# A dense layer stream issued in paced portions beside pair attention, with constant products in thinly filled slots

## The chip, the cores and the metric

The kernel runs on one core of a Trainium2 chip. The metric is the device time of one execution in microseconds. A core has five engines that work side by side, each with its own instruction queue: TensorE (PE, matrix products; PEld are its weight loads), VectorE (DVE), ScalarE (ACT), GpSimd (POOL) and SyncE (SP, which here issues the DMA transfers). Each queue runs in order, and an instruction that waits holds everything behind it on its engine.

## The reference, cut to what matters

Two layers are computed on x of 4 x 1024 tokens with 256 channels. The first (a recurrent mixer and a mixture of experts) is the first 1100 us and is not touched. The second is pair attention and a dense feed-forward layer, and the change is in how these two are interleaved.

```python
def _L1_attn_ref(X, Wq, Wk, Wphi, Wy_w, Wy_b, We_w, We_b):
    q = jnp.einsum('bnc,ac->bna', X, Wq)
    k = jnp.einsum('bnc,ac->bna', X, Wk)
    Vy = jnp.einsum('bnc,dc->bnd', X, Wy_w) + Wy_b
    e = jax.nn.relu(_rho_signed_sqrt(q[:, :, None, :] + k[:, None, :, :]))
    scores = jnp.einsum('bija,a->bij', e, Wphi)
    m = jnp.max(scores, axis=-1, keepdims=True)
    ex = jnp.exp(scores - m)
    ...
def _L1_ffn_ref(x, ...):                       # D_IN 256, D_HID 1024
    h = jax.nn.silu(_tlin(x, w1_w, w1_s)) * _tlin(x, w2_w, w2_s)
    h = jax.nn.gelu(_tlin(h, h1_w, h1_s), approximate=False)
    h = jax.nn.gelu(_tlin(h, h2_w, h2_s), approximate=False)
    return _tlin(h, w3_w, w3_s)
...
x = x + ga * _L1_attn_ref(h, ...)
h = _layernorm(x, axis=-1) * (1 + cb) + sb
x = x + gb * _L1_ffn_ref(h, ...)
```

## The kernel before, in words

**Blocks and turns.** pair_attention() handles 128 score blocks of 32 queries against all 1024 keys of a batch entry, 32 blocks for each of the four entries. A block is 16 tiles of 128 x 1024 in 8 pairs. Its loop runs 8 turns, p = 0 to 7, and each turn does one pair of the current block: weigh() on DVE (L1478, two passes over 128 x 1024), then work(ROOM[p]), then begin() and make() for a pair some 13 turns ahead. begin() puts the key sums on POOL (L1402, L1407), make() puts the others on ACT (L1427) or DVE (L1416), takes the square root on ACT (L1428) and the scores on PE (L1432, sixteen 32-column products). RING = 14 buffers hold the pairs between begin() and weigh(), so POOL can start a pair only when DVE has weighed one.

**The ends of a block.** At p = 5 top() takes the row maximum of the next block's scores (L1442, then a small product L1445 across partitions), at p = 6 exps() reads it (L1449), takes the exponential on ACT (L1451), and spread() copies the result over partitions on PE (L1458). exps() ends with switch(), which runs the Silu and Gelu activations that are waiting (L1375), so that ScalarE changes its function table only there: once in 8 turns.

**Work beside the blocks.** work(room) first calls tick(), which runs evictions whose LATE = 2 turns have passed, then takes generators from two lists, tasks and stream, until room is used up. A generator yields what it has issued, in units of one product of 128 x 128 by 256 columns, or nothing when it wants to wait a turn. ROOM is (4, 6, 6, 6, 6, 4, 3, 6). tasks holds finish(), which every four blocks puts the attention's output together (L1491, L1529, L1541; 14 units). stream holds first_rest() (the rest of the first layer), prepare() for each further batch entry, and dense(j) for the 16 groups of 256 tokens. Two PSUM banks serve all of these; banks[0] counts the free ones. finish() holds one for about eight turns.

**A dense group** goes through five matrices: W1 (16 units, gate() and first_products(), L1263, scaled by L1255, then Silu), W2 (16 units, multiplied with the Silu by L1298), H1 and H2 (64 units each, L1333, scaled by L1317, then Gelu), W3 (16 units, L1354, L1364, the sum L1365 and the store L1366). Activations sit in two tiles wide[0] and wide[1]; the input of W1 and W2 lies in a quarter of wide[1], and so the gate is split over both tiles. Between the matrices the group waits until its evictions are issued (while late) and its activation has run (while waiting). While a group is in H2, head() of the following one loads its tokens (L1268), normalises them (L920 to L947) and issues the first half of W1; the other half follows in dense().

**Weights** come in 512 KB tiles through weights() (L1047, on SP's queue), up to three ahead in four buffers. W1 and W2 are two tiles each, H1 and H2 eight each, W3 two.

A group can start when finish() has written its 256 tokens, every eight blocks. There is no other limit on the stream's speed than ROOM, the banks and the waits.

Of the kernel before, what the change touches and what calls it, by code (L numbers as in the profile page):

```python
# [14 lines left out]
P = 128  # L15
# [11 lines left out]
FB = 256  # L27
# [5 lines left out]
ROOM = (4, 6, 6, 6, 6, 4, 3, 6)  # L33
LATE = 2
ADDS = ('ap', 'pp', 'pp', 'dp', 'pp', 'ap', 'dp', 'ap')
# [799 lines left out]
def pair_attention(tc, a, link, out, cols_of, seen, ident):  # L835
# [14 lines left out]
    with tc.tile_pool(name="at_k", bufs=1) as pk, tc.tile_pool(name="at_w", bufs=1) as wp, tc.tile_pool(  # L850
# [31 lines left out]
        ewt, ews = [], []  # L882
        for i in range(2):
            t = wp.tile([P, 4, P], F32, tag=f"ewt{i}", name=f"ewt{i}")
            nc.gpsimd.memset(t, 0.0)
            ewt.append(t)
            t = wp.tile([P, 4, 64], F32, tag=f"ew{i}", name=f"ew{i}")
            nc.gpsimd.memset(t, 0.0)
            ews.append(t)
# [354 lines left out]
        def gate(j, m):  # L1244


            while not banks[0]:
                yield
            hT, to = wide[1][:, 0:2, :], (wide[1][:, 4 + m : 6 + m, :] if m < 4 else wide[0][:, m : m + 2, :])
            ps = bank([P, 2, FB], "ff_ps")  # L1250
            first_products(ps, weights(j, W1 + m // 4, 1 if m < 4 else 3), m, hT)
            if m % 4 == 2:
                used(j, W1 + m // 4)
            scale = fs[:, m : m + 2, 0:1].to_broadcast([P, 2, FB])
            later(LATE, lambda: nc.vector.tensor_tensor(to, ps, scale, ALU.mult))  # L1255
            yield 4

        def first_products(ps, w, m, hT):
# [6 lines left out]
        def head(j):  # L1265

            heads[j] = tokens[j] = p2.tile([P, 2, C], F32, tag="res", name="res")
            nc.sync.dma_start(tokens[j], dst[j].rearrange("(t p) c -> p t c", p=P))  # L1268
            yield
            yield  # L1270
            yield from normed(tokens[j], 2, j * FB // T, 3, wide[1][:, 0:2, :])
            for m in (0, 2):
                yield from gate(j, m)
# [4 lines left out]

        def dense(j):
# [3 lines left out]
            hT, gate_row = two[:, 0:2, :], rows[b]  # L1283
            if j not in heads:
                yield from head(j)
            for m in (4, 6):
                yield from gate(j, m)
            while late:
                yield
            between(two[:, 4:8, :], AF.Silu)  # L1290
            between(one[:, 4:8, :], AF.Silu)
            while waiting:
                yield

            def up(ps, m):
                for h in range(2):
                    g = two[:, 4 + m + h, :] if m < 4 else one[:, m + h, :]
                    nc.vector.scalar_tensor_tensor(  # L1298
                        one[:, m + h, :], ps[:, h, :], fs[:, m + h, 1:2], g, ALU.mult, ALU.mult
                    )  # L1300

            for m in range(0, 8, 2):
# [3 lines left out]
                first_products(ps, weights(j, W2 + m // 4), m, hT)  # L1306
# [3 lines left out]
                yield 4  # L1310
            while late:
                yield
            following = None
            for li, base, of, to in ((2, H1, one, two), (3, H2, two, one)):

                def hidden(ps, m):
                    nc.vector.tensor_tensor(  # L1317
                        to[:, m : m + 2, :], ps, fs[:, m : m + 2, li : li + 1].to_broadcast([P, 2, FB]), ALU.mult
                    )

                if li == 3 and follower() is not None:
                    following = head(follower())
                    next(following)
                for m in range(0, 8, 2):
                    if m == 4 and following is not None:
                        next(following)
# [14 lines left out]
                while late:  # L1341
                    yield
                between(to, AF.Gelu)
                if following is not None:
                    yield from following
                while waiting:
                    yield
            while not banks[0]:
                yield
            ps = bank([P, 2, C], "out_ps")  # L1350
            w = [weights(j, W3 + i).rearrange("p (k n) -> p k n", k=4) for i in range(2)]
# [9 lines left out]
            def last():  # L1361
                fin, res = two[:, 2:4, :], tokens.pop(j)
# [384 lines left out]
```

## Time and profile before

| | us |
|---|---|
| median of 3 runs | 4834.72 (4834.62 to 4846.67) |
| profiled execution | 4844.85, its span 4843.1 |
| first L1451 (block 0) to last L1451 (block 127) | 1109.3 to 4671.1 |
| mean granted TensorE clock over the span | 0.915 |
| L1432 scores, PE, 16384 instructions | 1169.6 busy |
| L1333 H1 and H2, PE, 4096 instructions | 999.1 busy |
| L1478 weighing, DVE, 2048 passes | 2393.1 busy |
| L1428 square roots, ACT, 1024 | 1928.6 busy |
| L1402 and L1407, POOL | 1600.0 and 1421.4 busy |

A product in f32 is two MATMUL instructions, so 4096 of L1333 are 2048 products. In the rows of the profile each group of instructions is named by line, engine, operation, output and inputs; after the bar or in brackets stands how long the engine was idle before it and which engine released it. Spans of busy engines overlap, and the clock column is the share of full clock that TensorE was granted.

### The profile page before, as it was taken

The page shows a single profiled execution, that of the slowest core. Times are in us where ns is not written, and L with a number is a line of the kernel's source. Part 1 is how long each engine was busy: PE and PEld are TensorE (multiplying, and loading weights), DVE is VectorE, ACT ScalarE, POOL GpSimd, SP SyncE. Part 2 cuts the span into 40 slices and gives each one's busy share as a digit, 9 for nine tenths or more (in the row PEclk, how much of TensorE's full clock was granted, in tenths as well). Part 3 has the DMA queues.
Part 4 walks back from the last instruction along what each step waited for, and adds up shares of the span by engine and source line. Part 5 has one row for each costly group of instructions (what it writes and reads, how often), then busy time and mean ns, then how long its engine had stood idle before and what let it go on. Part 6 is the DMA issues. An engine that isn't in the chain of part 4 may idle for free. (4 is left out here: it accounts for less than half of the span.)

```text
span 4843.1 us, 76620 instructions
## 1 busy us (share of the span) xinstructions
PE 4253.5 (88%) x28714; PEld 2423.4 (50%) x28714; DVE 3881.2 (80%) x6834; ACT 3316.7 (68%) x3183; POOL 3573.9 (74%) x2942
## 2 busy tenths in 40 slices
PE   6899999986888889899897889898889899998888
PEld 1233333433335446555564556555446555555567
DVE  5899999767898888778877878878788878878771
ACT  2333233227888898778878878888788888878851
POOL 3544444337899898889888888888898888888840
PEclk8799999987889889999998999999899999999999
DMA  4344333441112123322222332222223322222223
GB/s 137 91 120 118 107 112 108 128 140 34 33 63 68 63 73 102 105 93 81 79 86 56 109 108 83 85 79 81 66 82 105 106 86 83 77 77 75 78 86 116
DMA packets 256965, 433.16 MB, mean 89 GB/s; under 512 B 71897, under 2 KB 142737, under 8 KB 256337
## 3 DMA queue, kind: packets, MB, share of 16 engines
q1 hardware_dynamic: 253520, 425.76, 28.3%
q8 instruction: 226, 3.70, 0.3%
q10 hardware_dynamic: 2880, 1.98, 0.1%
q14 instruction: 147, 1.20, 0.1%
q0 software_dynamic: 192, 0.52, 0.0%
HBM read 403.99 MB, written 40.93 MB: 92 GB/s over the span
## 5 line engine op out<-in xcount | busy, mean ns | idle before, releaser
L1478 DVE CUSTOM_DVE_ANT_0 s<-s,xb 128x1024 f32<-128x1024 f32 x2048 | 2393.1, 1213 | 63.9 <-PE xb L1458 47.1
L1428 ACT ACTIVATE s<-s 128x2048 f32<-128x2048 f32 x1024 | 1928.6, 1908 | 174.1 <-POOL s L1407 104.6
L1402 POOL TENSOR_SCALAR s<-kB,qt 128x1024 f32<-128x1024 f32 x1397 | 1600.0, 1151 | 281.8 <-DVE ew L1478 108.4
L1407 POOL TENSOR_SCALAR s<-s 128x1024 f32<-128x1024 f32 x1016 | 1421.4, 1399 | 89.1
L1432 PE MATMUL sc<-s,wsel 128*32 128x256 f32 x16384 | 1169.6, 411 | 332.8 <-ACT s L1428 331.6
L1333 PE MATMUL ff_ps<-wide,fw 128*128 128x256 f32 x4096 | 999.1, 393 | 25.1 <-ACT wide L1375 23.7
L1432 PEld LDWEIGHTS sc<-s,wsel 128*32 128x32 f32 x16384 | 456.7, 114 | 903.2 <-ACT s L1428 500.4
L1333 PEld LDWEIGHTS ff_ps<-wide,fw 128*128 128x128 f32 x4096 | 762.8, 193 | 231.3 <-issue 102.5
L741 POOL TENSOR_TENSOR kv<-vb,out_k 128x512 f32<-128x512 f32 x256 | 324.0, 1274 | 244.0 <-DVE state L809 167.4
L1427 ACT ACTIVATE s<-kB,qt 128x1024 f32<-128x1024 f32 x387 | 439.9, 1137 | 18.6 <-DMA kB<-kd 18.1
L616 PE MATMUL e_ps<-wd,hid 128*128 128x512 f32 x896 | 417.8, 613 | 7.0 <-DVE acc L599 4.5
L1458 PE MATMUL xb<-ex,pick 64*128 64x256 f32 x2048 | 320.8, 436 | 46.2 <-ACT ex L1451 46.0
L809 DVE TENSOR_TENSOR_SCAN state<-dec,carry,kv 128x512 f32<-128x512 f32 x256 | 326.2, 1274 | 23.4 <-ACT dec L796 17.5
L616 PEld LDWEIGHTS e_ps<-wd,hid 128*128 128x128 f32 x896 | 170.9, 196 | 233.1 <-issue 219.2
L1416 DVE TENSOR_SCALAR s<-kB,qt 128x1024 f32<-128x1024 f32 x264 | 285.9, 1085 | 0.0
L1263 PE MATMUL ff_ps<-wide,fw 128*128 128x256 f32 x1024 | 268.0, 411 | 17.7 <-DMA fw<-in_ffw_dram 17.0
L1458 PEld LDWEIGHTS xb<-ex,pick 64*128 64x128 f32 x2048 | 193.2, 204 | 180.2 <-ACT ex L1451 80.0
L1317 DVE TENSOR_TENSOR wide<-ff_ps,ffn_s 128x512 f32<-128x512 f32 x128 | 88.0, 687 | 212.2 <-PE ff_ps L1333 212.2
L1442 DVE TENSOR_REDUCE sc<-sc 128x1 f32<-128x256 f32 x128 | 55.1, 431 | 249.0 <-PE sc L1432 248.4
L801 ACT COPY carry<-state 128x1 f32<-128x1 f32 x255 | 47.9, 188 | 295.6 <-DVE state L809 295.3
L1263 PEld LDWEIGHTS ff_ps<-wide,fw 128*128 128x128 f32 x1024 | 200.2, 204 | 79.7 <-issue 35.9
L1451 ACT ACTIVATE ex<-sc,neg 128x256 f32<-128x256 f32 x128 | 60.7, 474 | 254.0 <-DVE neg L1449 252.6
(254 smaller groups left out, 4155.1 us busy)
## 6 DMA issues: line engine op xcount, KB each, us to landing
fw<-in_ffw_dram SPq DMA_DIRECT2D x361, 512.0 KB
vb<-vd SPq DMA_DIRECT2D x1024, 64.0 KB
lent<-vd SPq DMA_DIRECT2D x64, 514.0 KB
wd<-in_w_down_dram SPq DMA_DIRECT2D x28, 1024.0 KB
kB<-kd SPq DMA_DIRECT2D x32, 512.0 KB
lent<-in_We_dram SPq DMA_DIRECT2D x32, 512.0 KB
kd<-nd SPq DMA_DIRECT2D x24, 512.0 KB
vd<-out_v SPq DMA_DIRECT2D x8, 512.0 KB
```

The costliest lines, as they stand in the source:

```text
L616: nc.tensor.matmul(ps, hid[:, k, t * P : (t + 1) * P], wd[:, k, :], start=k == 0, stop=k == HID // P - 1)
L741: nc.gpsimd.tensor_mul(kv, vb[:, g % 2, :], ready[u]["k"][:, n // HN, :])
L809: nc.vector.tensor_tensor_scan(s[:, 1 : U + 1], dec, kv, c, ALU.mult, ALU.add)
L1263: nc.tensor.matmul(ps[:, h, :], w[:, k, o : o + P], hT[:, k, :], start=k == 0, stop=k == 1)
L1333: nc.tensor.matmul(ps[:, h, :], w[:, k * P : (k + 1) * P], of[:, k, :], start=k == 0, stop=k == 7)
L1402: nc.gpsimd.tensor_scalar(self.s[p][:, h, :], kB[self.b][i % 8], 1.0, self.query(i), ALU.mult, ALU.add)
L1407: nc.gpsimd.tensor_scalar(both, both, FLT_MAX, 0.0, ALU.min, ALU.max)
L1427: nc.scalar.activation(t[:, h, :], kB[self.b][i % 8], AF.Relu, bias=self.query(i))
L1428: nc.scalar.activation(t, t, AF.Sqrt, bias=EPS_RHO)
L1432: nc.tensor.matmul(self.sc[32 * j : 32 * j + 32, 0:256], wsel[:, g, 16 * (1 - s) : 16 * (1 - s) + 32], t[:, h, 256 * j : 256 * (j + 1)], s ...
L1458: nc.tensor.matmul(xb[:, 256 * j : 256 * (j + 1)], pick[q, j % 2, s, :], self.ex[q, :], start=True, stop=True)
L1478: nc.vector.tensor_tensor_reduce(t[:, h, :], t[:, h, :], self.xb[s], 1.0, 0.0, ALU.mult, ALU.add, ew[:, self.n % 4, col : col + 1])
```

## The change

It has four parts. The four gates of W1 are issued in one go, gates(), for the following group behind H2, in the same stretch; their input is a tile hT of its own, all of wide[1] holds the gate, and its Silu waits for the same switch() as H2's Gelu. The stream is paced: even() divides a layer's units by the turns up to a switch(), and work() gives the stream only as much as rate and credit allow; EVEN, HALF and HURRY bound the rate, HURRY when work is waiting or near the end. head() runs in a list of its own, side. And work() adds products on constants (ident times pick, or times zeros into the score tile) in turns where fewer than LEAST = 2 units were issued, while scores are still being made. Besides, one ewt tile instead of two, and the last scaling, sum and store in two halves.

```diff
--- before.py
+++ after.py
@@ -31,7 +31,9 @@
 RING = 14
 PREP = 12
 ROOM = (4, 6, 6, 6, 6, 4, 3, 6)
+EVEN, HALF, HURRY = 4.2, 3.3, 5.0
 LATE = 2
+LEAST = 2
 ADDS = ('ap', 'pp', 'pp', 'dp', 'pp', 'ap', 'dp', 'ap')
 FIRST_ON_SCALAR = 6
 LEAD = 2
@@ -879,11 +881,10 @@
         same = wp.tile([P, P], F32, tag="same", name="same")
         part = wp.tile([P, 4], F32, tag="part", name="part")
         pick = wp.tile([P, 2, 2, P], F32, tag="pick", name="pick")
-        ewt, ews = [], []
+        ewt, ews = wp.tile([P, 4, P], F32, tag="ewt", name="ewt"), []
+        nc.gpsimd.memset(ewt, 0.0)
+        hT = wp.tile([P, 2, FB], F32, tag="hT", name="hT")
         for i in range(2):
-            t = wp.tile([P, 4, P], F32, tag=f"ewt{i}", name=f"ewt{i}")
-            nc.gpsimd.memset(t, 0.0)
-            ewt.append(t)
             t = wp.tile([P, 4, 64], F32, tag=f"ew{i}", name=f"ew{i}")
             nc.gpsimd.memset(t, 0.0)
             ews.append(t)
@@ -1241,21 +1242,26 @@
 
         groups, heads, tokens = {}, {}, {}
 
-        def gate(j, m):
-
-
-            while not banks[0]:
-                yield
-            hT, to = wide[1][:, 0:2, :], (wide[1][:, 4 + m : 6 + m, :] if m < 4 else wide[0][:, m : m + 2, :])
-            ps = bank([P, 2, FB], "ff_ps")
-            first_products(ps, weights(j, W1 + m // 4, 1 if m < 4 else 3), m, hT)
-            if m % 4 == 2:
-                used(j, W1 + m // 4)
-            scale = fs[:, m : m + 2, 0:1].to_broadcast([P, 2, FB])
-            later(LATE, lambda: nc.vector.tensor_tensor(to, ps, scale, ALU.mult))
-            yield 4
-
-        def first_products(ps, w, m, hT):
+        def gates(j, n):
+
+            for m in range(0, 8, 2):
+                while not banks[0]:
+                    yield
+                ps = bank([P, 2, FB], "ff_ps")
+                first_products(ps, weights(j, W1 + m // 4, min(n, n + 1 - m // 4)), m)
+                if m % 4 == 2:
+                    used(j, W1 + m // 4)
+
+                def gated(ps=ps, m=m):
+                    scale = fs[:, m : m + 2, 0:1].to_broadcast([P, 2, FB])
+                    nc.vector.tensor_tensor(wide[1][:, m : m + 2, :], ps, scale, ALU.mult)
+                    if m == 6:
+                        between(wide[1], AF.Silu)
+
+                later(LATE, gated)
+                yield 4
+
+        def first_products(ps, w, m):
             w = w.rearrange("p (k n) -> p k n", k=2)
             for h in range(2):
                 o = (m + h) % 4 * P
@@ -1264,66 +1270,79 @@
 
         def head(j):
 
-            heads[j] = tokens[j] = p2.tile([P, 2, C], F32, tag="res", name="res")
+            tokens[j] = p2.tile([P, 2, C], F32, tag="res", name="res")
             nc.sync.dma_start(tokens[j], dst[j].rearrange("(t p) c -> p t c", p=P))
             yield
             yield
-            yield from normed(tokens[j], 2, j * FB // T, 3, wide[1][:, 0:2, :])
-            for m in (0, 2):
-                yield from gate(j, m)
+            yield from normed(tokens[j], 2, j * FB // T, 3, hT)
 
         def follower():
 
             return groups.get(stream[1]) if len(stream) > 1 else None
+
+        def even(units, most=EVEN, less=2):
+
+            t = turns[0]
+            end = t + 1 + (6 - t) % 8
+            if sum(g in groups for g in stream) > 2 or any(g not in groups for g in stream) or t > 8 * (N - 12):
+                most = HURRY
+            while units > most * (end - t - less):
+                end += 8
+            rate[0] = units / (end - t - less)
+            credit[0] = rate[0]
+
+        rate, credit, side = [0.0], [0.0], []
 
         def dense(j):
 
             b = j * FB // T
             one, two = wide
-            hT, gate_row = two[:, 0:2, :], rows[b]
+            gate_row = rows[b]
             if j not in heads:
+                heads[j] = True
                 yield from head(j)
-            for m in (4, 6):
-                yield from gate(j, m)
-            while late:
-                yield
-            between(two[:, 4:8, :], AF.Silu)
-            between(one[:, 4:8, :], AF.Silu)
-            while waiting:
+                even(16)
+                yield from gates(j, 3)
+                rate[0] = 0.0
+            while late or waiting:
                 yield
 
             def up(ps, m):
                 for h in range(2):
-                    g = two[:, 4 + m + h, :] if m < 4 else one[:, m + h, :]
                     nc.vector.scalar_tensor_tensor(
-                        one[:, m + h, :], ps[:, h, :], fs[:, m + h, 1:2], g, ALU.mult, ALU.mult
+                        one[:, m + h, :], ps[:, h, :], fs[:, m + h, 1:2], two[:, m + h, :], ALU.mult, ALU.mult
                     )
 
+            rate[0] = EVEN
             for m in range(0, 8, 2):
                 while not banks[0]:
                     yield
                 ps = bank([P, 2, FB], "ff_ps")
-                first_products(ps, weights(j, W2 + m // 4), m, hT)
+                first_products(ps, weights(j, W2 + m // 4), m)
                 if m % 4 == 2:
                     used(j, W2 + m // 4)
                 later(LATE, lambda ps=ps, m=m: up(ps, m))
                 yield 4
+            rate[0] = 0.0
             while late:
                 yield
-            following = None
+            follow = None
             for li, base, of, to in ((2, H1, one, two), (3, H2, two, one)):
 
                 def hidden(ps, m):
                     nc.vector.tensor_tensor(
                         to[:, m : m + 2, :], ps, fs[:, m : m + 2, li : li + 1].to_broadcast([P, 2, FB]), ALU.mult
                     )
-
-                if li == 3 and follower() is not None:
-                    following = head(follower())
-                    next(following)
+                    if m == 6:
+                        between(to, AF.Gelu)
+
+                if li == 3:
+                    follow = follower()
+                if follow is not None:
+                    heads[follow] = True
+                    side.append(head(follow))
+                even(*((64, EVEN) if follow is None else (80, HALF, 4)))
                 for m in range(0, 8, 2):
-                    if m == 4 and following is not None:
-                        next(following)
                     while not banks[0]:
                         yield
                     ps = bank([P, 2, FB], "ff_ps")
@@ -1338,17 +1357,18 @@
                         used(j, base + m + h)
                     later(LATE, lambda ps=ps, m=m: hidden(ps, m))
                     yield 2
-                while late:
-                    yield
-                between(to, AF.Gelu)
-                if following is not None:
-                    yield from following
-                while waiting:
+                if follow is not None:
+                    while side:
+                        yield
+                    yield from gates(follow, 1)
+                rate[0] = 0.0
+                while late or waiting:
                     yield
             while not banks[0]:
                 yield
+            rate[0] = EVEN
             ps = bank([P, 2, C], "out_ps")
-            w = [weights(j, W3 + i).rearrange("p (k n) -> p k n", k=4) for i in range(2)]
+            w = [weights(j, W3 + i, 2 - i).rearrange("p (k n) -> p k n", k=4) for i in range(2)]
             for t in range(2):
                 for k in range(8):
                     nc.tensor.matmul(
@@ -1359,13 +1379,16 @@
             used(j, W3), used(j, W3 + 1)
 
             def last():
-                fin, res = two[:, 2:4, :], tokens.pop(j)
+                res = tokens.pop(j)
                 heads.pop(j)
-                nc.vector.tensor_tensor(fin, ps, gate_row[:, 1:2, :].to_broadcast([P, 2, C]), ALU.mult)
-                nc.gpsimd.tensor_add(res, res, fin)
+                for t in range(2):
+                    fin = p2.tile([P, C], F32, tag="ln_xn", name="fin")
+                    nc.vector.tensor_tensor(fin, ps[:, t, :], gate_row[:, 1, :], ALU.mult)
+                    nc.gpsimd.tensor_add(res[:, t, :], res[:, t, :], fin)
                 nc.sync.dma_start(out[j * FB : (j + 1) * FB, :].rearrange("(t p) c -> p t c", p=P), res)
 
             later(LATE, last)
+            rate[0] = 0.0
             yield 2
 
 
@@ -1491,7 +1514,7 @@
                 nc.tensor.transpose(ps[:, m, :], ew[:, m, :], ident)
             yield
             yield
-            z = ewt[i % 2]
+            z = ewt
             for u in range(2):
                 for s in range(2):
                     r = 64 * u + 32 * s
@@ -1566,12 +1589,14 @@
         def work(room):
 
 
+            least = room - LEAST
             tick()
             turns[0] += 1
+            credit[0] = min(credit[0] + rate[0], 8.0)
             if issues and turns[0] % 2:
                 issues.pop(0)()
-            for of in (tasks, stream):
-                while of and room > 0:
+            for of in (tasks, side, stream):
+                while of and room > 0 and (of is not stream or not rate[0] or credit[0] > 0):
                     got = next(of[0], self_done)
                     if got is self_done:
                         of.pop(0)
@@ -1579,6 +1604,19 @@
                         break
                     else:
                         room -= got
+                        if of is stream:
+                            credit[0] -= got
+            if made < 8 * N and room > least:
+                rhs = pick.rearrange("p j s m -> p (j s m)")[:, 0:256]
+                if banks[0]:
+                    ps = bank([P, 256], "idle")
+                    for _ in range(room - least):
+                        nc.tensor.matmul(ps, ident, rhs, start=True, stop=True)
+                    banks[0] += 1
+                elif made % 8:
+                    nothing = wsel[:, 0, 0:1].to_broadcast([P, 256])
+                    for _ in range(room - least):
+                        nc.tensor.matmul(blocks[made // 8].sc[:, 0:256], ident, nothing, start=False, stop=False)
 
         def begin():
             nonlocal begun
@@ -1641,6 +1679,7 @@
             if n % 4 == 3:
                 tasks.append(finish(n, ew, exT))
         while tasks or stream:
+            credit[0] = 16.0
             work(16)
             switch()
         while late:
```

## The prediction

> **What bounds the kernel now.** I first read the busy shares on the page, then the engines' busy time by stage.
>
> ```profile
> PE 4253.5 (88%) x28714; PEld 2423.4 (50%) x28714; DVE 3881.2 (80%) x6834; ACT 3316.7 (68%) x3183; POOL 3573.9 (74%) x2942
> ```
> ```profile
> 1430.00:4671.00 3241.00, 2867.05 (x23353) 1785.82 (x23354) 2659.33 (x4839) 2706.28 (x2051) 2820.11 (x2298) 0.92 0.26 84
> 4694.00:4843.10 149.10, 127.96 (x554) 108.93 (x552) 19.28 (x38) 16.16 (x16) 4.35 (x5) 0.93 0.37 123
> ```
>
> Columns of the second: window, length, then busy PE, weight loads, DVE, ACT, POOL, granted clock, DMA share, GB/s. The change acts from about 1430 us on, where the first dense group starts. From 1430 to 4671 lie 116 score blocks (start of L1451 to start of L1451), 27.94 us each; per block PE is busy 24.7, POOL 24.3, ACT 23.3, DVE 22.9. No engine is full; the question is why a block takes 3 us more than its busiest engine. After 4694 only dense work is left, and PE alone carries it.
>
> ```profile
> DVE sc L1442 <- PE sc L1432: 212.2, 67, 8.6
> DVE wide L1317 <- PE ff_ps L1333: 119.3, 41, 5.4
> DVE neg L1449 <- PE sc L1445: 82.2, 67, 8.8
> ```
> ```profile
> 4397.00:4423.00 26.00, 19.37 (x181) 10.17 (x184) 22.96 (x44) 21.99 (x17) 24.55 (x21) 0.83 0.20 66
> ```
>
> The first are DVE's waits within that window: 414 us in three rows, all on a PE that is late. The second is a block with 9 dense units: PE has room, POOL is busy 24.55 of 26.0. So a light block is POOL's, at about 25.3 us, and dense work costs what makes PE late beyond that. I call one 128x128x256 f32 product (two MATMULs) a unit.
>
> ```profile
> 2546.04 3.64 PE L1354 MATMUL out_ps<-fw,wide 128*128 128x256 f32 x8 [1.15 <-ACT wide L1375]
> ...
> 2550.61 2.86 PE L1354 MATMUL out_ps<-fw,wide 128*128 128x256 f32 x12
> ```
> ```profile
> 1974.67 6.01 PE L1263 MATMUL ff_ps<-wide,fw 128*128 128x256 f32 x16 [5.92 <-DMA fw<-in_ffw_dram]
> ...
> 1982.04 0.16 DVE L1449 TENSOR_REDUCE neg<-sc 128x1 f32<-128x4 f32 x1 [8.83 <-PE sc L1445]
> ```
> ```profile
> 4766.18 27.79 PE L1333 MATMUL ff_ps<-wide,fw 128*128 128x256 f32 x128
> ...
> 4798.03 29.58 PE L1333 MATMUL ff_ps<-wide,fw 128*128 128x256 f32 x128 [4.06 <-ACT wide L1375]
> ```
>
> From the timeline: after a Gelu PE is cold (8 MATMULs in 3.64 us, where 12 take 2.86); a weight tile that lands late stops PE for 5.92 us and DVE for 8.83; alone, 64 units take 27.79 us, 0.434 each.
>
> **Sorting the blocks.** Leaving out 12 blocks around the three prepare() (29.33 us each), I counted each block's units and whether a Gelu stop falls in it. Without one: under 20 units 25.35 us (25 blocks), 20 to 29 27.13 (21), 30 to 37 27.79 (21), 38 and more 29.37 (12). With one: under 20 29.42 (2), 20 to 29 28.54 (9), 30 to 37 28.69 (4), 38 and more 31.94 (10).
>
> **Part 1, the pacing: how much dense work is left at the end.** This is arithmetic on turns (8 per block). After a Gelu stop W3 and the next W2, 16 units each at 4.2 a turn, with two waits of LATE turns, end 11 turns on. H1 asks 64/4.2 = 15.2 turns and 2 spare, so it ends with the stop 32 turns after the first. H2 with the next gates asks 80/3.3 = 24.2 and 4 spare: 32 turns. A group takes 64 turns. Under HURRY 80/5 + 4 = 20 gives 24 turns, 56 in all, or 64 when a finish() takes the bank and the room and the stop is missed. Before, L1354 comes every 190 us, 6.8 blocks or 54 turns, when groups wait in line. A group becomes ready every 64 turns, but first_rest and three prepare() cost the stream some 20 blocks, and the slower stream never makes that up. Counted through all turns with ROOM, banks, loans and LATE, the old rules leave 272 units after the last block (the count puts every L1354 into the block in which the trace has it), the new ones 514. So 242 units move from the blocks into the end. **Price: 242 x 0.434 = +105.** Each of the 1.4 groups more brings its stops (last group: 87.4 us for 176 units, 11 over 0.434 each): +15. The head and gates of the last two groups, now behind H2, fill one wait each (PE stood 3 us for POOL's ln_xn before 4748.26, 4.06 at the Gelu of 4798): -14. End: **+106**, between +90 and +125.
>
> **Part 2, the blocks.** The same count sorts the new blocks: without a stop 21 under 20 units, 46 of 20 to 29, 10 of 30 to 37, 5 above; with one 4, 15, 3 in the last three classes; 12 around prepare(). At the class prices: 532 + 1248 + 278 + 147 + 114 + 430 + 96 + 352 = 3197, against 3241: **-44**. The new portions come 2 to 4 a turn instead of 6 and then none, which the class prices don't know. If the 46 middle blocks fell to POOL's 25.5, that would be 46 x 1.6 = -74 more; at worst 0. I take half, -37. Three old light blocks hold the late weight tile at 8 to 9 us each (key loads stood before it in SP's queue); at 3 units a turn a tile lasts 2.8 turns and the tile ahead hides that: 0 to -24, I take -15.
>
> **Part 3, queues passed.** The old gates asked for W2's tiles with W1's second, ahead of the out store. The new one asks with W2's first product, behind that store in SP's queue, which waits for DVE's L1364, POOL's add and its own 0.40 us. By the DMA packets of 31 loads that had the queue to themselves, a 512 KB tile is complete 3.0 us after issue. So 0.96 (two halves of 0.48 at L1298's row) + 0.78 (L1553's) + 0.4 + 3.0 = 5.1 us after DVE starts, and more if POOL is behind; behind the W2 product in PE wait that turn's scores and the L1445 product, for which DVE's L1449 waits. DVE has two turns of its own work meanwhile (some 6 us): 0 to 5 us for each of 12 groups. I take 2: **+25**, bounds 0 and 60. W1's tiles come one at a time, but their buffers are free a whole tile earlier: 0, hidden by the last H2 tile (8 units, 2.8 turns), 3 us each if not. The head (res load, L920, L921, the ACT root, two POOL L931, four transposes, two L947) goes from H2's second half to its start, same count: 0, before paced products that don't need it.
>
> **Part 4, activations.** Silu shares the Gelu's stop: 15 stops fewer, already outside the classes; a fit of all 116 blocks gives 0.6 us each, -9. ACT then holds Gelu, Silu (1.91 instead of two of 1.05) and perhaps one table load (1.28) before the next root, +0.6 in 10 stops: +6. Together **-3**.
>
> **Part 5, products on constants.** The count has 608 of them, 263 us of PE. They stand in turns where PE has L1432 (1.07) and little else out of POOL's 3.1 us: +0.86 and a switch of 0.33 make 2.3, so 0 while PE is on time. Where it is late each costs 0.43: at most some +40 for those around finish(). Their gain: without the cold clock, W3's and H2's first products save up to 1.7 at each of 25 stops, -42. I take **-10**. The Trainium skill ("TensorE: Matmul & The Clock Gate", Part 1) says that the gate halves the clock after an idle window of about 3.4 us; this trace has half speed after stops of 2 to 4 us. By that rule the fill before the stop would spare most of them, an estimate of -40. The same page (Part 3, "What overlaps and what doesn't") says that matmuls never pass each other, which speaks against filling: a fill that waits for a bank holds the scores behind it. The 8.83 us above agree.
>
> **At nothing.** One ewt: the next copies come 32 turns after its reader; hT of its own; two halves in last(): 0.27 us more on DVE and on POOL per group, in DVE's idle time.
>
> **Sum.** +106 - 44 - 37 - 15 + 25 - 3 - 10 = +22, and +5 for finish() colliding with hurried portions: about +27 on the span of 4843.1. The execution took 4844.85, 10.1 above the median, so 4834.7 + 27 = **4862**.
>
> **Rivals.** (a) Faster: portions as even as the rate says free DVE's 414 us of waits to more than half. Then light and middle blocks stand at 25.3 to 25.5, stops cost 2: stage at 26.4, 116 x 1.54 = -179, with +106 gives 4762; with half of it 4810. For it: those waits, and PE's need in a block staying below POOL's time up to 30 units (12.2 us for scores at 8 x 1.2, L1458 at 2 x 1.1 and L1465 at 0.4, with 0.432 per unit). Against: 33 new blocks still hold 30 or more. Chance 0.30, from 4770 to 4820. (b) No change: gain and tail cancel within 0.3%, about what a measurement tells apart (the three runs spread by 0.25%). 0.11. (c) Much slower: the late W2 tile at each group. At 8.83 us for 12 groups it is +106 instead of +25: 4943. It decides from 6 us of stall per group. Against: DVE's two turns of slack. 0.13. (d) The pacing doesn't act, because credit is loose or room binds first: then no units move and the time stays at 4835. Against: 80 units in 32 turns is far below ROOM's 41 a block. 0.02, counted with (b). The forecast, slower by 0.3 to 1.6%, has 0.44 with (c) apart.
>
> Faster 0.30, same 0.13, slower 0.57. The range reaches from (a)'s middle to (c): **4765 to 4945**; the forecast's own is 4850 to 4910.
>
> **What would show it.** After the last L1478 the end should last 240 to 270 us instead of 149, with 2 to 3 groups in it; L1354's counterpart should come every 64 turns; blocks from 1430 on should average 27.0 to 27.4. L1442's wait on PE well under 100 us and blocks near 26.3 would show (a). Waits of the W2 products on a DMA, a dozen times 3 us and more, would show Part 3. An end near 150 us would break Part 1 and with it the forecast.

## The result and the profile after

| | before | after |
|---|---|---|
| median of 6 runs each, us | 4840.52 (4834.62 to 4846.71) | 4930.05 (4926.61 to 4937.81) |
| ratio, 95% interval | | 1.0186 [1.0173, 1.0199] |
| profiled execution, its span | 4844.85, 4843.1 | 4929.48, 4927.7 |
| block 0 to block 11, by the start of the exponentials | 320.4 | 322.1 |
| block 11 to block 127 ("stage" below) | 3241.4 | 3200.8 |
| block 127 to the end ("end" below) | 172.0 | 300.9 |

The change makes the kernel 1.9% slower. The blocks gained 41 us and the end lost 129 (after the last weighing: 149 before, 271 now). Forecast were a gain of 79 in the blocks (Parts 2 to 5 and the 5 us for finish()) and 106 more at the end.

The page of the changed kernel, engines' busy time, and then its windows (length; busy PE, weight loads, DVE, ACT, POOL; granted clock, DMA share, GB/s) for the blocks and for the time after the last weighing:

```profile
PE 4446.7 (90%) x29894; PEld 2554.6 (52%) x29894; DVE 3890.1 (79%) x6850; ACT 3320.3 (67%) x3169; POOL 3577.6 (73%) x2957
```
```profile
1426.00:4627.00 3201.00, 2933.28 (x23884) 1804.52 (x23880) 2651.50 (x4816) 2693.74 (x2026) 2819.71 (x2307) 0.97 0.24 78
4657.00:4927.70 270.70, 234.00 (x1028) 200.53 (x1028) 36.94 (x75) 30.72 (x27) 7.12 (x11) 0.95 0.38 126
```

DVE, ACT and POOL do what they did. PE is busy 193 us longer over the span with 1180 MATMUL instructions more (those on constants), and its clock in the blocks rose from 0.92 to 0.97. In the blocks PE is busy for 92% of the time. The second window shows the moved work: 1028 MATMULs after the last weighing instead of 554, so 237 more units; 242 were counted.

The waits of the changed kernel in the blocks (waiting engine and line, releaser, sum, count, largest), and behind them the one for W3's products in the kernel before:

```profile
DVE sc L1465 <- PE sc L1455: 211.3, 89, 14.7
PE sc L1455 <- ACT s L1451: 174.0, 125, 5.3
DVE wide L1333 <- PE ff_ps L1352: 68.2, 30, 4.0
DVE fin L1386 <- PE out_ps L1374: 66.2, 12, 9.8
DVE neg L1472 <- PE sc L1468: 57.2, 59, 6.5
PE ff_ps L1269 <- DMA fw<-in_ffw_dram: 40.1, 13, 6.9
```
```profile
DVE wide L1364 <- PE out_ps L1354: 31.8, 8, 5.1
```

L1465 is the row maximum, L1333 the evictions of H1 and H2, L1386 the last scaling, L1472 the second maximum. The evictions do what pacing promised (119.3 before), but the largest row, the wait for the scores, stands at 211 as before, with a largest single wait of 14.7 instead of 8.6; the waits for W3's products grew from 31.8 to 66.2, and PE waits 13 times for a weight tile at L1269, the line of both W1 and W2. Nine of these, of 3.25 to 6.89 us and 35.1 together, are W2's; the other four, of 0.5 to 1.7 us, are W1's (DVE's L1257, the gate, takes their products).

The blocks show it one by one. 53 of the 116 are now under 26 us (36 before). But nine blocks in which W3 and the next W2 fall take 35.3 to 43.2 us: 33, 41, 61, 69, 77, 96, 103, 111 and 119. Block 96 is the worst. Its timeline, SP's queue and then the engines (start, duration, engine, line, operation, count; in brackets the idle time before and the releaser):

```profile
3781.40 0.40 SPq L1388 DMA_DIRECT2D out_dram<-res  x1
3781.85 0.46 SPq L1527 DMA_DIRECT2D xr<-x  x1
3782.36 0.99 SPq L1533 DMA_DIRECT2D lent<-vd  x2
3783.46 1.67 SPq L1048 DMA_DIRECT2D fw<-in_ffw_dram  x3
```
```profile
3779.45 0.76 DVE L1386 TENSOR_TENSOR fin<-out_ps,mrows 128x256 f32<-128x256 f32 x2 [9.77 <-PE out_ps L1374]
...
3789.37 3.75 PE L1269 MATMUL ff_ps<-hT,fw 128*128 128x256 f32 x8 [6.89 <-DMA fw<-in_ffw_dram]
3793.06 1.77 PE L1455 MATMUL sc<-s,wsel 128*32 128x256 f32 x16
...
3794.97 0.43 DVE L1465 TENSOR_REDUCE sc<-sc 128x1 f32<-128x256 f32 x1 [10.21 <-PE sc L1455]
...
3798.77 0.48 ACT L1474 ACTIVATE ex<-sc,neg 128x256 f32<-128x256 f32 x1 [9.85 <-DVE neg L1472]
```

From DVE's start at L1386 to the out store on SP it takes 1.95 us (scaling and sum come in two halves, the store is one, behind both), then three loads of finish() go ahead, 2.06 more to the issue of the weights, and 5.91 from there until the first W2 product runs. PE stands 6.89, the products after it run at half speed (8 in 3.75), the scores behind them come late, and DVE and ACT wait 10 us in turn. Block 77 shows the same without finish() in the way:

```profile
3254.01 0.75 DVE L1386 TENSOR_TENSOR fin<-out_ps,mrows 128x256 f32<-128x256 f32 x2 [4.42 <-PE out_ps L1374]
...
3256.41 1.90 SPq L1048 DMA_DIRECT2D fw<-in_ffw_dram  x4
...
3260.45 1.97 PE L1269 MATMUL ff_ps<-hT,fw 128*128 128x256 f32 x8 [3.41 <-DMA fw<-in_ffw_dram]
...
3263.77 0.16 DVE L1472 TENSOR_REDUCE neg<-sc 128x1 f32<-128x4 f32 x1 [3.68 <-PE sc L1468]
```

### The profile page after: what moved, and what is told of

It reads as the page before. It is cut to its first block, busy times and chain, and to the rows that moved or that the text cites. A ratio compares the mean times of both kernels' runs of the same rounds, so it can differ in the third digit from the quotient of the medians.

```text
span 4927.7 us, 79069 instructions
## 1 busy us (share of the span) xinstructions
PE 4446.7 (90%) x29894; PEld 2554.6 (52%) x29894; DVE 3890.1 (79%) x6850; ACT 3320.3 (67%) x3169; POOL 3577.6 (73%) x2957
## 5 line engine op out<-in xcount | busy, mean ns | idle before, releaser
L1455 PE MATMUL sc<-s,wsel 128*32 128x256 f32 x16384 | 1129.9, 395 | 205.1 <-ACT s L1451 203.6
L1352 PE MATMUL ff_ps<-wide,fw 128*128 128x256 f32 x4096 | 1009.9, 392 | 37.8 <-ACT wide L1398 33.4
L1352 PEld LDWEIGHTS ff_ps<-wide,fw 128*128 128x128 f32 x4096 | 747.9, 191 | 257.9 <-issue 120.6
L1455 PEld LDWEIGHTS sc<-s,wsel 128*32 128x32 f32 x16384 | 437.0, 111 | 765.4 <-ACT s L1451 325.1
L1269 PE MATMUL ff_ps<-hT,fw 128*128 128x256 f32 x1024 | 276.5, 421 | 63.0 <-DMA fw<-in_ffw_dram 61.1
L1481 PE MATMUL xb<-ex,pick 64*128 64x256 f32 x2048 | 294.6, 407 | 21.1 <-ACT ex L1474 21.1
L1614 PE MATMUL idle<-pick,ident 128*128 128x256 f32 x1032 | 297.3, 412 | 0.7 <-DVE wide L1257 0.7
L618 PEld LDWEIGHTS e_ps<-wd,hid 128*128 128x128 f32 x896 | 171.1, 196 | 233.4 <-issue 219.6
L1333 DVE TENSOR_TENSOR wide<-ff_ps,ffn_s 128x512 f32<-128x512 f32 x128 | 87.7, 685 | 238.3 <-PE ff_ps L1352 238.2
L1269 PEld LDWEIGHTS ff_ps<-hT,fw 128*128 128x128 f32 x1024 | 205.3, 209 | 124.7 <-issue 53.0
L1465 DVE TENSOR_REDUCE sc<-sc 128x1 f32<-128x256 f32 x128 | 55.3, 432 | 253.0 <-PE sc L1455 250.9
L1481 PEld LDWEIGHTS xb<-ex,pick 64*128 64x128 f32 x2048 | 178.5, 188 | 141.4 <-issue 65.0
```

What stands on the lines that cost most here:

```text
L618: nc.tensor.matmul(ps, hid[:, k, t * P : (t + 1) * P], wd[:, k, :], start=k == 0, stop=k == HID // P - 1)
L1269: nc.tensor.matmul(ps[:, h, :], w[:, k, o : o + P], hT[:, k, :], start=k == 0, stop=k == 1)
L1352: nc.tensor.matmul(ps[:, h, :], w[:, k * P : (k + 1) * P], of[:, k, :], start=k == 0, stop=k == 7)
L1455: nc.tensor.matmul(self.sc[32 * j : 32 * j + 32, 0:256], wsel[:, g, 16 * (1 - s) : 16 * (1 - s) + 32], t[:, h, 256 * j : 256 * (j + 1)], s ...
L1481: nc.tensor.matmul(xb[:, 256 * j : 256 * (j + 1)], pick[q, j % 2, s, :], self.ex[q, :], start=True, stop=True)
```

## The experiments

**Theory:** the pacing itself is about neutral (the end loses what the blocks gain), and two side effects make the loss: W2's tiles behind the out store, and the products on constants. **Rivals:** pacing is the whole loss; the blocks of W3 are dear because of their two activations; the constants pay through the clock. All times are medians, stage and end are of the profiled execution; each ratio is to the kernel before in the same session. A stop is a switch() at which waiting activations run and the dense stream stands until they are done.

**1. W2's tiles early.**

```diff
 used(j, W3), used(j, W3 + 1)
+if follow is not None:
+    weights(follow, W2, 2)
```

> The changed kernel, but the two W2 tiles of the following group are asked for right after W3's products, ahead of the out store in SP's queue. Theory (late tile): the W2 products lose their waits of 3.4 to 6.9 us on the DMA, 12 times in the blocks and 3 times at the end. At 3 to 5.5 us of block time each that is 36 to 66 us, and 15 to 20 at the end: 4930 falls to 4845 - 4880. Rival (W3's blocks are dear for other reasons: two activations with a table load each, finish() in the same block): the waits go, but the time falls by less than 20, to 4910 or more. Rival (constants or pacing alone): no change, 4925 - 4935.

Measured: 4859.71, ratio 1.0042 [1.0027, 1.0057], so 70 us less than after. The nine waits for W2's tiles are gone, the four for W1's stay. The stage is 3149.6 (-51), the end 277.7 (-23). The nine blocks named above fell by 3.4 to 9.9 us each, 51.8 together, which is the whole gain of the stage. The three other blocks with a W3 (19, 48, 84), where no gates stand behind H2, changed by 0.7 at most. The same place of block 96 in this kernel:

```profile
3757.82 0.76 DVE L1388 TENSOR_TENSOR fin<-out_ps,mrows 128x256 f32<-128x256 f32 x2 [9.31 <-PE out_ps L1374]
...
3760.78 1.99 PE L1269 MATMUL ff_ps<-hT,fw 128*128 128x256 f32 x8
...
3763.92 0.43 DVE L1467 TENSOR_REDUCE sc<-sc 128x1 f32<-128x256 f32 x1 [0.77 <-PE sc L1457]
```

The eight products run without a wait, warm (at the full clock), in 1.99 us, and DVE's 10.21 are 0.77. The wait for W3's products (9.31) is still there. In the changed kernel's last groups the wait stood quite open:

```profile
4645.63 9.93 PE L1269 MATMUL ff_ps<-hT,fw 128*128 128x256 f32 x32 [6.96 <-DMA fw<-in_ffw_dram]
4749.22 9.34 PE L1269 MATMUL ff_ps<-hT,fw 128*128 128x256 f32 x32 [6.44 <-DMA fw<-in_ffw_dram]
...
4842.26 8.91 PE L1269 MATMUL ff_ps<-hT,fw 128*128 128x256 f32 x32 [6.49 <-DMA fw<-in_ffw_dram]
```

**2. No products on constants.**

```diff
-LEAST = 2
+LEAST = 0
```

> The changed kernel without the products on constants (LEAST = 0). Theory (the constants neither help nor hurt much; the loss is the end and the late tile): 4915 - 4945, the granted clock in the blocks falls from 0.97 towards 0.92. Rival (constants stand in PE's way, above all around prepare() and finish()): 4870 - 4910. Rival (they warm the clock, as a rule of an idle window would have it): 4960 - 4990.

Measured: 4882.77, ratio 1.0089 [1.0074, 1.0104], 47 less than after. The stage is 3158.6 (-42), the end 300.5 as in the changed kernel, where no constants fall after the last scores. The mean granted clock over the span fell from 0.952 to 0.921: a lower clock and a faster kernel. The rival that expected them in the way was right.

**3. No pacing.**

```diff
-EVEN, HALF, HURRY = 4.2, 3.3, 5.0
+EVEN, HALF, HURRY = 100.0, 100.0, 100.0
```

> The changed kernel with EVEN, HALF and HURRY at 100, so that ROOM bounds the stream again; gates behind H2, constants and the queue order stay. Theory: the end after the last weighing shrinks from 270 to 150 - 190 us, but the blocks give back the evenness (some 70 to 110 us) and keep the late W2 tile: 4880 - 4930. Rival (pacing is the whole loss): 4830 or less. Rival (pacing is no part of it): within 10 of 4930.

Measured: 4938.76, ratio 1.0199 [1.0182, 1.0217]. The end went back to 171.4, and the stage up to 3334.2, by 133, more than the 70 to 110 expected. Pacing alone is not the loss; the total is where the second rival put it (within 10 of 4930), because stage and end cancel and not because pacing does nothing.

**4. The constants alone, in the kernel before.**

```diff
+            if made < 8 * N and room > least:
+                rhs = pick.rearrange("p j s m -> p (j s m)")[:, 0:256]
...
```

> The kernel before with the products on constants alone. Theory: a small effect, 4825 - 4850 against 4840.5. Rival (constants are in the way): 4870 - 4910. Rival (they warm the clock and pay): 4790 - 4815.

Measured: 4912.76, ratio 1.0147 [1.0132, 1.0162], 72 slower than before, above even the rival's span. Blocks 22, 54 and 86, where prepare() works, went from 32.20 to 38.77 us each: 20 of the stage's 66 us; the rest is spread over many blocks. Why is best seen in block 22 of the changed kernel, beside the same block before; windows as above, then PE's timeline:

```profile
1729.40:1761.60 32.20, 30.41 (x228) 15.76 (x220) 22.15 (x39) 25.45 (x22) 30.38 (x27) 1.00 0.28 74
```
```profile
1727.10:1765.90 38.80, 38.80 (x265) 21.36 (x268) 21.29 (x38) 25.55 (x23) 31.36 (x27) 1.00 0.24 66
```
```profile
1729.27 2.00 PE L989 MATMUL q_ps<-lent,wide 128*128 128x64 f32 x16
1731.11 1.08 PE L1614 MATMUL idle<-pick,ident 128*128 128x256 f32 x4
1732.12 1.07 PE L1455 MATMUL sc<-s,wsel 128*32 128x256 f32 x16
1733.12 1.93 PE L1003 MATMUL k_ps<-wide,lent 128*64 128x512 f32 x4
1734.98 1.13 PE L1614 MATMUL idle<-pick,ident 128*128 128x256 f32 x4
```

PE is busy for all of the 38.80 us, at full clock. prepare() issues 2 us of products (L989, L1003) and then yields nothing instead of a number, so work() takes the turn for an empty one and adds two units on constants. Sixteen units in eight turns keep PE busy 8.4 us more. It had 1.8 us idle in this block before, and the block is 6.6 longer: all that PE had no room for. The price depends on the block. In the changed kernel blocks 51, 52, 87 and 88, where the other two prepare() work, hold 14 or 16 units each and are 2.3 to 3.5 us longer than in e2, although PE has 2.8 to 8.2 us idle there in e2; block 86 holds 16 too and takes 27.65 us, 27.64 in e2, where PE is busy for 18.5 of it.

**5 to 8. Both repaired, and what pacing is worth then.** Each is the changed kernel with the edits of 1 and 2, and one more:

```diff
 e6: EVEN, HALF, HURRY = 100.0, 100.0, 100.0
 e7: EVEN, HALF, HURRY = 4.2, 4.6, 5.5      and  even(..., (80, HALF, 6))
 e8: while late or waiting: yield
+    yield
```

> The changed kernel with W2's tiles asked for ahead of the out store (as in e1) and without products on constants (as in e2). If the two losses are separate they add: 4930 - 70 - 47 = 4813, within 8, which is below the kernel before. Rival (both stand in the same stops, and each repairs the other's): 4840 - 4860.

> As e5, and EVEN, HALF and HURRY at 100, so that ROOM bounds the stream. Theory (the pacing alone is near nothing net: what the blocks gain, the end loses): 4800 - 4840, the end near 150 after the last weighing, the blocks some 130 longer in all than in e5. Rival (pacing is a gain once the other two losses are gone): above 4850. Rival (pacing is a loss of its own): below 4790.

> As e5, with H2 and the next gates spread over 24 turns instead of 32 (HALF 4.6, HURRY 5.5, six turns spare instead of four). Counted through the turns this leaves 316 units to the end instead of 514: 198 x 0.434 = 86 less there. Theory (a unit moved into a block that POOL sets costs less than 0.434, one above 37 units costs about as much): 30 to 60 of the 86 are given back in the blocks, so 4757 - 4787 if e5 is 4813. Rival (each unit costs the same in a block as at the end): equal to e5.

> As e5, and the stream lets one turn pass after each stop for its activations before it issues the next products, so that PE doesn't stand behind two table loads and two activations with that turn's scores behind it. In e1's profile DVE waited 68.2 us in 12 rows for W3's products and the scores behind them. Theory (double stop): 20 - 50 less than e5. Rival (the products are late by a turn and the evictions with them; the stop moves, not its cost): within 8 of e5.

| run | median us | ratio to before | stage | end |
|---|---|---|---|---|
| e5 | 4818.30 | 0.9951 [0.9934, 0.9968] | 3114.8 | 277.3 |
| e6, no pacing | 4817.25 | 0.9946 [0.9930, 0.9963] | 3214.4 | 171.1 |
| e7, quicker | 4769.73 | 0.9855 [0.9840, 0.9871] | 3165.7 | 178.8 |
| e8, a turn's rest | 4857.83 | 1.0035 [1.0021, 1.0050] | 3140.5 | 289.7 |

e5 is where the two losses add (4813 expected). e6 against e5 is the pacing by itself: the stage gains 100, the end loses 106, and the medians differ by 1. (The profiled execution of e6 was 10 us below its median, so the stage may gain up to 110.) e7 keeps half of the stage's gain with an end only 8 us longer than without pacing, and beats both kernels, 1.45% under the one before. Windows of e6, e5 and e7, blocks and then the time after the last weighing:

```profile
1420.00:4634.00 3214.00, 2851.01 (x23415) 1783.20 (x23416) 2654.10 (x4852) 2702.38 (x2036) 2827.58 (x2314) 0.93 0.26 84
4657.00:4805.40 148.40, 125.66 (x539) 106.73 (x538) 18.05 (x37) 13.74 (x13) 4.63 (x7) 0.94 0.32 109
```
```profile
1425.00:4540.00 3115.00, 2743.33 (x22908) 1664.12 (x22908) 2653.14 (x4818) 2694.34 (x2026) 2822.80 (x2308) 0.94 0.25 81
4570.00:4817.30 247.30, 226.24 (x1008) 194.88 (x1006) 34.79 (x69) 29.27 (x23) 7.12 (x11) 0.96 0.41 134
```
```profile
1422.00:4587.00 3165.00, 2825.70 (x23296) 1746.29 (x23296) 2657.08 (x4844) 2705.89 (x2033) 2825.64 (x2313) 0.94 0.26 84
4615.00:4765.90 150.90, 134.43 (x604) 116.11 (x603) 20.18 (x40) 17.19 (x13) 4.62 (x7) 0.98 0.38 125
```

e8 was a miss: DVE's wait for W3's products (1430 to 4560 us) fell from 62.8 us in e5 to 28.7, but its wait for the scores rose from 152 to 223, and the end grew by 12. The turn of rest cost 40.

**9, 12, 10. Which constants cost.** e9 and e12 split e1's 590 products on constants by a condition in work(): a dense group alone in hand, or not. e10 puts the first sort into e7.

```diff
-if made < 8 * N and room > least:
+if made < 8 * N and room > least and not (tasks or side) and stream and stream[0] in groups:
```

> As e1 (W2 early, paced), with products on constants only in turns where a dense group alone is in hand: 210 of e1's 590, mostly around the stops. Between e1 (4860) and e5 (4818) lie 42 us. Theory (the loss comes where finish() and prepare() have issued products that they don't count, so that work() takes a full turn for an empty one): 4810 - 4822. Rival (each product on a constant costs the same): 210/590 of 42 is 15, so 4833. Rival (the clock rule holds, filled stops are spared): below 4800.

> The complement of e9: as e1, with products on constants only in the other turns, where finish(), prepare(), head() or the first layer's rest is in hand: 380 of 590. Theory: nearly all of the 42 us stay, 4853 - 4866. Rival (each the same): 27 of 42, 4845.

> As e7 (4770), with the 226 products on constants in turns where a dense group alone is in hand. If a warm clock after the stops pays: 4740 - 4762. If it doesn't: 4765 - 4780.

Measured: e9 4822.00 (ratio 0.9966 [0.9952, 0.9979]), e12 4844.19 (1.0007 [0.9998, 1.0016]), e10 4790.37 (0.9897 [0.9883, 0.9910]). Of the 42 us between e5 and e1, 26 come back with the 380 products beside finish(), prepare() and the first layer's rest and 4 with the 210 of the dense turns; the other 12 are about what the intervals leave open (4 to 8 us for each run). The theory had wanted 35 or more for e12. e12 by itself lies where the rival with one price for each product put it (4845), e9 does not (4833): so where the products stand matters, but that uncounted products are the reason is shown in block 22 and not for the whole sum. In e12 block 22 is at 38.77 again, and blocks 51, 52, 87 and 88 of the other two prepare() are 1.5 to 2.8 longer than in e5. e10 is 21 above e7, outside both of its spans: in the turns around the stops, where a warm clock should have paid, the products cost time too.

**11, 13, 14. The wait for W3's products.** e11 is e7 with the last scaling one turn later; e13 spreads the portions anew and keeps that; e14 is e13 without it.

```diff
 e11, e13: later(LATE + 1, last)
 e13, e14: EVEN, HALF, HURRY = 4.8, 5.0, 5.5;  even(64, EVEN, 3) and even(80, HALF, 5)
```

> As e7, with the scaling of W3's output on DVE one turn later (LATE + 1). In e7's profile DVE stands 87 us in 14 rows for W3's products, 6 us each. If these waits set the blocks: 4720 - 4750. If POOL or the bank that is held a turn longer sets them: 4765 - 4785.

> As e5, with EVEN 4.8, HALF 5.0, HURRY 5.5, three turns spare in H1 and five in H2 with the next gates, and the scaling of W3's output one turn later. The count of turns leaves 310 units to the end, where the same count gives 514 for e11, and 9 blocks above 37 units instead of 13 in e7. Theory (e11 lost by a missed stop, not by the later scaling; DVE's wait for W3's products is worth 20 to 40 us): end 175 - 185 us, total 4715 - 4750. Rival (the later scaling itself costs, through the bank it holds): 4800 or more. Rival (DVE's wait is hidden): as e14.

> As e13 without the later scaling (LATE as it was): 308 units to the end by the count. Theory (evenness at the same number of units left): 4745 - 4770, a little below e7's 4770. Rival: as e13.

Measured: e11 4836.56 (0.9989 [0.9980, 0.9998]), e13 4802.08 (0.9928 [0.9913, 0.9942]), e14 4816.82 (0.9955 [0.9943, 0.9967]). DVE's wait for W3's products in the blocks, e7 and then e11:

```profile
DVE fin L1388 <- PE out_ps L1374: 87.0, 14, 9.2
```
```profile
DVE fin L1388 <- PE out_ps L1374: 19.8, 11, 2.0
```

The wait went as meant, and the kernel was 67 us slower: e11's stage is 3128.6, its end 279.8 against 178.8. The end is that of e5: counted through the turns, one turn more in each group makes groups miss a stop, and a missed stop is eight turns (514 units left instead of 316). The traces agree: e7's W3 comes in blocks 32, 39, 46 and 52, e11's in 32, 40, 48 and 60, and behind the start of block 127's exponentials stand 336 dense units in e7 and 528 in e11. e13, with the stops restored, has an end of 185.8 again and keeps the later scaling. Against e14 it is 15 better, less than the 20 to 40 expected, and so the later scaling itself does not cost. Both missed their spans (4715 to 4750 and 4745 to 4770) and lie above e7, though e14 leaves as many units to the end (308 counted, 316 in e7) and has an end of 185.0: its stage is 3198.3, with blocks 37, 69, 101 and 125 at 35.6 to 38.5. Why that order of portions is dearer than e7's wasn't tried further.

## Why the prediction was right in direction and wrong in size

The forecast was +27 us, the measured change +89.5. Two steps failed: Part 3, whose price was too small, and Part 5, whose sign was wrong. Step by step, each with what the runs give for it:

| step | forecast | measured | from |
|---|---|---|---|
| Part 1, the end | +106 | +106 | end, e6 to e5 |
| Part 2, blocks, evenness, late tiles | -96 | -100 | stage, e6 to e5 |
| Part 3, W2's tiles behind the out store | +25, 0 to 60 | +64 to +70 | e2 to e5, after to e1 |
| Part 5, products on constants | -10, up to +40 | +42 to +47 | e1 to e5, after to e2 |
| Part 4 and the edits at nothing | -3 | -24 | before to e6 |
| collision with finish() | +5 | not separated | |

In one order they close: -24 (before to e6), +1 (e6 to e5), +112 (e5 to after), together +89. Against the forecast Part 3 is 45 dearer (by e1) and Part 5 52 (by e5); Part 4 and the edits at nothing gave 21 back, the pacing 9, and 5 were set down for finish().

- **Part 1 and Part 2 were right**, in sign and in size, the second by luck: I took half of a possible evenness gain. Sorted by the dense units in the traces, leaving out the blocks around prepare(), e5 has 52 blocks with 20 to 29 units and no Gelu stop, at 25.5 us in the mean (35 at 27.4 before, 16 at 26.9 in e6). That is the best case of Part 2, and so the other classes together did worse than forecast. Of the signs, the end (270 us) and groups seven or eight blocks apart came; the blocks average 27.6 us and not 27.0 to 27.4, because of Parts 3 and 5. That the change slows the kernel is not due to them: they cancel.
- **Part 3 is a mis-sized term.** The mechanism is the one named, and the sign that was to show it (W2 products waiting for a DMA a dozen times) is there: nine times in the blocks and three times at the end, 3.25 to 6.96 us each. Three things were off. The stretch from L1386 to the first product was put at 5.1 us; in block 77 it is 6.4 (3254.01 to 3260.45, of which 4.0 from the issue of the weights instead of 3.0), and in block 96 it is 9.9, because finish()'s loads stand between the store and the weights and are still under way when these are issued. The sum also stopped at the first W2 product. The eight products and the scores behind it, which it names, got no time: 3.3 us until DVE goes on in block 77 (3260.45 to 3263.77), and 5.6 in block 96, at half speed. The cover, DVE's own work "meanwhile (some 6 us)", was there: DVE works until 3260.08 in block 77, 6.1 us, and 5.3 us in block 96. But the whole way takes 9.8 and 15.5 us, and DVE waits the rest, 3.68 and 10.21. And the end's groups, with nothing at all beside them, were not priced: three waits of 6.4 to 7.0. So 51.8/9 = 5.8 us for each of nine groups and 23 at the end stand in place of 2 for each of 12. W1's tiles, put at 0, were late five times, 6.2 us of PE in all. Rival (c) put 8.83 on each of 12 groups and gave 4943, 13 from the measured time; that is luck, for its late tiles are 64 to 70 of its 106, and Part 5 makes up the rest.
- **Part 5 failed by its sign.** "They stand in turns where PE has L1432 and little else" was read off the code's count of units. A generator that issues products and yields no number looks empty to that count, and so block 22's sixteen units went in beside a PE that had 30.4 us of work in 32.2. The forecast's +40 for the bad case named finish() and not prepare(). prepare()'s five blocks (22, 51, 52, 87, 88) are 17 of the 46 us from after to e2; where the rest arises stays open. The gain of 42 set against it didn't come: at the stop of block 96 the fill runs at 3754.67, and after the wait of 5.31 us the products are cold all the same (12 of W3 in 4.32 us, 2.86 when warm).
- **Part 4 and the rest** gained 21 more than forecast. Which edit did it wasn't separated. The table load that it called "perhaps" is there: Silu and Gelu do not share a table. ScalarE's timeline at the stop of block 96, and then PE's:

```profile
3756.08 1.28 ACT L1398 ACT_TABLE_LOAD   x1
3757.37 1.91 ACT L1398 ACTIVATE wide<-wide 128x2048 f32<-128x2048 f32 x1
3759.30 1.28 ACT L1398 ACT_TABLE_LOAD   x1
3760.60 1.91 ACT L1398 ACTIVATE wide<-wide 128x2048 f32<-128x2048 f32 x1
3762.53 1.28 ACT L1451 ACT_TABLE_LOAD   x1
```
```profile
3765.78 1.94 PE L1455 MATMUL sc<-s,wsel 128*32 128x256 f32 x16 [5.31 <-ACT s L1451]
3767.65 4.32 PE L1374 MATMUL out_ps<-fw,wide 128*128 128x256 f32 x12
```

Each has a load of its own, and the roots a third: 7.7 us until the next root begins, for which PE's scores waited 5.31.

- **The rivals.** (a) wanted a stage of 26.4 us a block; without the two losses e5 has 26.85, and of the 127 us under before 27 are there in e6 without pacing. So the portions bring some 100 of its 179 us, and the wait for the scores fell from 207 us to 152 (1430 to 4560 us). Its 4810 "with half of it" doesn't come out of its own sum: half of 179 against 106 is 4851, slower than before, and so no case of a faster kernel. (b) and (d) fell: 237 units did move, and the block times changed throughout.
- **The clock rule.** The Trainium skill ("TensorE: Matmul & The Clock Gate", Part 1) says that an idle window of about 3.4 us halves the clock, and by it the fill was worth an estimated 40 us. For long waits the runs agree: after 6.89 us eight products took 3.75 us, and 1.99 without the wait. As a threshold they don't confirm it: in the kernel before eight products of L1458 took 2.08 us at 2542.82 after only 2.07 us of waiting, and 1.13 at 2554.40. The fill did raise the granted clock of the blocks, from 0.94 in e5 to 0.98 in e1. The stage still became 35 us longer: in block 22, 6.6 of them, the fill stands in PE's queue ahead of the scores and nothing passes it. The sentence of the same page that spoke against filling (Part 3, "What overlaps and what doesn't": matmuls never pass each other) was the one to price.

## What to carry to other kernels

A filler that is added "where nothing was issued" must count instructions, not the units that generators report (block 22); and a higher granted clock is no gain by itself, the stage's length is. When a step moves in a program, follow the loads that it asks for past everything that now stands ahead of them in the issuing queue, and price the wait also in the tail, where nothing covers it. Evening out work pays only if the same amount still ends in time: in e11 groups missed an eight-turn stop, which cost 101 us at the end, as much as e5's even portions had won in the blocks.

## What the hardware showed

- Silu and Gelu in one stop need a table load each (1.28 us), and the activation starts 0.01 to 0.02 us after its load ends.
- A 512 KB tile that is asked for with others just behind it is later than the 3.0 us of single loads: 4.0 from issue to product in block 77 (four tiles issued from 3256.41 on, product at 3260.45), 5.9 in block 96 (three, behind three loads of finish()).
- Four MATMULs on constants at 3780.34, and the sixteen of the scores behind them, did not keep PE warm across the wait of 6.89 us that ended at 3789.37: the products after it ran at half speed (8 in 3.75 us).
- Filling raises the granted clock and can still cost time: 0.921 over the span without the constants and 4883 us (e2), 0.952 with them and 4930 (after).
